# A tiled key projection ahead of the scores, its eviction ahead of the last exponentials, another projection behind the maxima's transposes, and the context loaded by pieces

## The chip, the core and the metric

The kernel runs on one core of one Trainium2 chip. The metric is the device time of one execution in microseconds (us); the time given is the median of several runs. A core has five engines that run beside each other and wait for each other by semaphores: PE (TensorE, the matmuls), DVE (VectorE), ACT (ScalarE), POOL (GpSimd) and SP (SyncE, which here only starts transfers). Each engine works through its own list of instructions in order: one that waits holds up all that are behind it on its engine.

## What is computed

One layer of a Perceiver, in fp32, on 32 batches of 64 query rows of width 256 and a context of 1601 rows of width 256, 16 heads of 16:

```
x = x + cross_attention(layernorm(x), ctx)     # softmax over 1601 keys, all 32 x 16 x 64 rows of scores
x = x + span_attention(layernorm(x))           # weights exp(-soft*(pos-mean)^2), 64 positions
x = x + ffn(layernorm(x))                      # a shared gated part and two of eight experts a token
```

The cross attention holds most of the work: keys and values are projected from the context (`ctx @ wk.T + bk`, `ctx @ wv.T`), then for each head `softmax(q @ k.T / 4) @ v`.

## The kernel before

**Stages.** A short prologue loads weights and prepares batch 0. The main loop (L767) goes over 63 *halves*: half n is batch b = n // 2 and c = n % 2, that is one set of eight heads of one batch. After it come the last half, the rest of the feed-forward's first part and the experts.

**Layout.** The context lies transposed. A batch's 1601 keys are 13 blocks of 124, loaded as four pieces (`GROUPS`: blocks 0 to 3, 4 to 6, 7 to 9, 10 to 12) of 372 KB or so each into a ring of five buffers (`ct`, L146). Scores are held with keys on the partitions, in `prob`, as four pairs of heads a half (j = 0 to 3). Their maximum over the keys is found by running maxima over the 13 blocks on DVE (`mrun`, the last one writes `mx`), four transposes on PE (`pm`, L597), a reduction on DVE (`mc`, L604), and four transposes back that spread it over the partitions (`pb`, L612), which ACT copies to `mb` (L616).

**What a half does**, in the order in which the loop's body issues it. A software pipeline runs over three halves: in iteration n the values product belongs to half n-1, the subtraction of maxima and the exponentials to half n, the scores to half n+1, and the projections of keys (K0 to K3, one for each piece) and values (V0 to V6, two blocks each) to the next batch.

1. `values(n-1, 0)`: 52 matmuls (104 records) with the first two pairs of `prob`; then `exponentials(n-1, 3)`, ACT's fourth exponential of the half before.
2. `scores(n+1, 0)`: 16 matmuls, four PSUM banks; behind them `pm` of half n; DVE adds the mask (L573) and reduces `mc`.
3. `project_keys(c, 0)`: K0, two matmuls of 496 columns on PE and an eviction on ACT (L510); then `pb` and `mb`.
4. `less_maxima(n, 0)`, POOL's first subtraction (L621, 3.75 us each); `first_maxima` (ACT, L582); steps of the other stages (`run`); `values(n-1, 1)`, which needs the third and fourth exponential; running maxima on DVE.
5. `scores(n+1, 1)`; the first exponential; K1 and two value projections; the second subtraction; steps; the second exponential.
6. The third subtraction; `scores(n+1, 2)`; K2, K3 and one or two value projections, all tiled; the fourth subtraction; the third exponential; steps.

A tiled projection (`product`, L491) cuts the weights into strips of 32 columns at the four column positions of the PE array, so that the same product is 8 matmuls instead of 2.

**What sets the order.** PE, DVE, ACT and POOL run exactly in the order in which the code issues (`manual_schedule`, L733). The steps of the layer norm, the query projection and the span attention (`query_steps` L452, `span_steps` L245, `finish_steps` L706) are generators in an `agenda`; a table (`STEPS`, L232) says after how many thirds of a half each goes on. So the extra work comes in a cycle of four halves. In every fourth half ACT has, between its third exponential (L626) and the fourth, two normalisations (`xn_q`, `xn_h`, L215) and four span exponentials (L323).

**PSUM.** `mm_bank` (L108) hands out six banks in turn (`ps_x`, L395). Whoever takes a bank writes only when the last reader of the tenant six before is done. The readers are DVE for scores and ACT for projections, `pb` and the transposes.

**SP** issues transfers in order. `load_context` (L483) asks for all four pieces of batch b+1 at the start of the half (b, 0), and for the rows `x` of a later tile behind them; the pieces wait for their buffers, and `x_kept` (L382) is issued from the steps.

Of the kernel before, what the change touches and what calls it, by code (L numbers as in the profile page):

```python
# [33 lines left out]
GROUPS = [(0, 4), (4, 3), (7, 3), (10, 3)]  # L34
# [56 lines left out]
def perceiver_kernel(ctx: ExitStack, tc: tile.TileContext, a: dict[str, bass.AP], out: bass.AP):  # L91
    nc = tc.nc
    B = a["ctxT"].shape[0]
    NT = B * S
    NTILE = NT // P
# [12 lines left out]
    def mm_bank(name: str):  # L108
        return ps_mm.tile([P, 512], F32, tag="mm", name=name)
# [16 lines left out]
    def load_x(t: int):  # L126
        xs[t] = work.tile([P, D], F32, tag="x", bufs=5, name=f"x{t}")
        nc.sync.dma_start(out=xs[t], in_=a["x"][t * P : (t + 1) * P, :])
# [14 lines left out]
    def load_piece(b: int, g: int):  # L143
        c0, n = GROUPS[g]
        k0, kn = c0 * CHUNK, min(n * CHUNK, KEYS - c0 * CHUNK)
        ct = big.tile([P, 2, 4 * CHUNK], F32, tag="ct", bufs=5, name=f"ct_{b}_{g}")  # L146
        nc.sync.dma_start(
            out=ct[:, :, :kn],
            in_=a["ctxT"][b].rearrange("(c p) k -> p c k", p=P)[:, :, k0 : k0 + kn],
        )  # L150
        cts[b].append(ct)
# [328 lines left out]

        nc.gpsimd.tensor_tensor(xs[t], xs[t], bo_row, ALU.add)

    def load_context(b: int):  # L483
        for g in range(len(GROUPS)):
            load_piece(b, g)
        if b % 2 == 0 and b // 2 + 1 < NTILE:
            t = b // 2 + 1
            load_x(t)


    def product(out, lhsT, rhs, start: bool, stop: bool, tiled: bool):  # L491
        n = lhsT.shape[-1]
        for at in range(0, n, 32) if tiled else (0,):
            end = min(at + 32, n) if tiled else n
            nc.tensor.matmul(  # L495
                out[at:end], lhsT=lhsT[:, at:end], rhs=rhs, start=start, stop=stop,
                **(dict(tile_position=(0, at)) if tiled else {}),
            )
# [15 lines left out]
    def project_values(b: int, u: int, tiled: bool = False):  # L514

        blocks = range(2 * u, min(2 * u + 2, NKC))
        ps = mm_bank(f"pv_{b}_{u}")
        for n, k in enumerate(blocks):
            g = max(g for g in range(len(GROUPS)) if GROUPS[g][0] <= k)
            k0, kn = (k - GROUPS[g][0]) * CHUNK, min(CHUNK, KEYS - k * CHUNK)  # L520
            for i in range(2):
                product(
                    ps[:kn, n * D : (n + 1) * D], cts[b][g][:, i, k0 : k0 + kn], wvT[:, i, :],
                    i == 0, i == 1, tiled,
                )
        n = len(blocks)
        nc.scalar.copy(  # L527
            vs[b % 2][:kn, 2 * u : 2 * u + n, :, :DK],
            ps[:kn, : n * D].rearrange("p (n h d) -> p n h d", n=n, d=DK),
        )  # L530

    def scores(n: int, g: int, then=None, order=None):

        b, c = halves[n]
        c0, nb = SCORED[g]


        more = [mm_bank(f"psc_{b}_{c}_{g}"), spare_pvs] if nb == 5 else None
        pss = [mm_bank(f"psc_{b}_{c}_{g}_{j}") for j in range(4)]
        for r in range(nb):  # L540
            for j in range(4):
                e, s = divmod(j, 2)[::-1]
                fifth = nb == 5 and r == 4 * s
                i = 4 if fifth else r - (nb == 5 and s == 0)
                ps, at = (more[e], s) if fifth else (pss[j], i)
                if fifth and j == 2:
                    tc.add_manual_dep(nc.tensor.nop().ins, mm.ins.name, IN_TURN, reason="banks")
                k0 = (c0 + i) * CHUNK
                product = nc.tensor.matmul(  # L549
                    ps[:CHUNK, at * P : (at + 1) * P],  # L550
                    lhsT=kTs[c][32 * j : 32 * j + 32, k0 : k0 + CHUNK],
                    rhs=qbd[b // 2][32 * j : 32 * j + 32, c, b % 2, :, :],
                    start=True, stop=True, tile_position=(32 * j, 0),
                )
                if fifth and j == 1:
                    mm = product
        held = then() if then else None
        for item in (order or ORDER[g]).split():
            if item == "t":
                if held is not None:  # L560
                    maxima_of_rows(*held)
            elif item[0] == "m":
                maximum(n, int(item[1:]))
            elif item in "AB":
                k, e = c0 + 4, "AB".index(item)
                nc.vector.tensor_tensor(  # L566
                    block_of(n, k)[:, :, e, :],
                    more[e][:CHUNK, : 2 * P].rearrange("p (r q) -> p r q", r=2),
                    madd_fifth[:CHUNK, None, :].to_broadcast([CHUNK, 2, P]), ALU.add,
                )  # L570
            else:
                j = int(item)
                nc.vector.tensor_tensor(  # L573
                    pair_of(n, j)[:, c0 : c0 + 4, :].rearrange("p k (e q) -> p k e q", e=2),
                    pss[j][:CHUNK].rearrange("p (k e q) -> p k e q", k=4, e=2),
                    madd[:CHUNK, c0 : c0 + 4, None, :].to_broadcast([CHUNK, 4, 2, S]), ALU.add,
                )
# [24 lines left out]
    def maxima_of_rows(ps, col):  # L602

        nc.vector.tensor_reduce(  # L604
            col, ps[:, : 4 * CHUNK].rearrange("p (j k) -> p j k", j=4), AX.X, ALU.max
        )
# [18 lines left out]
    def exponentials(n: int, j: int):  # L625
        nc.scalar.activation(pair_of(n, j), pair_of(n, j), AF.Exp)  # L626

    def values(n: int, r: int):

        b, c = halves[n]  # L630
        v = vs[b % 2]
        for k in range(NKC):
            kn = min(CHUNK, KEYS - k * CHUNK)
            for j in range(4):
                h = 4 * r + j
                nc.tensor.matmul(  # L636
                    pvs[32 * j : 32 * j + DK + 1, c, :, r, :],
                    lhsT=v[:kn, k, 8 * c + h, :],
                    rhs=pair_of(n, h // 2)[:kn, k, (h % 2) * S : (h % 2) * S + S],
                    start=(k == 0), stop=(k == NKC - 1), tile_position=(0, 32 * j),  # L640
                )
# [119 lines left out]
    next(queries, None)  # L761
    for u in range(7):
        project_values(0, u)
    last = len(halves) - 1

    extra = {3 * last - 3: (0,), 3 * last - 2: (1, 2, 4), 3 * last - 1: (5, 6)}
    for n, (b, c) in enumerate(halves[:-1]):  # L767
        if c == 0 and b + 1 < B:
            load_context(b + 1)
        if c and b % 2 == 0 and b // 2 + 1 < NTILE:  # L770
            agenda[3 * n].append((b // 2 + 1, query_steps(b // 2 + 1)))

        def project(f, *args):
            if b + 1 < B:
                f(b + 1, *args)

        def steps(g: int):
            run(3 * n + g)
            for u in extra.get(3 * n + g, ()):
                linear_factor(u)  # L780

        def taken_off():
            turned.extend(turned_maxima(n))
            return turned

        turned: list = []
        if n:
            values(n - 1, 0)
            exponentials(n - 1, 3)
        scores(n + 1, 0, taken_off)  # L790
        project(project_keys, c, 0)
        m = maxima_along_rows(turned[1])
        less_maxima(n, 0, m, nc.gpsimd)
        held = 3 * n in held_at
        if not held:
            first_maxima(n + 1)
        run(3 * n)
        if n:
            values(n - 1, 1)
            if c == 0:  # L800
                agenda[3 * n + 1].append((b // 2, finish_steps(b - 1, 3 * n + 1)))
        for u in extra.get(3 * n, ()):
            linear_factor(u)
        if held:
            first_maxima(n + 1)
        else:
            for k in (1, 2) if c else (1, 2, 3):
                maximum(n + 1, k)

        scores(n + 1, 1, order=LATER if held else None if c else SOONER)  # L810
        exponentials(n, 0)
        project(project_keys, c, 1)
        for u in (4, 5) if c else (0, 1):
            project(project_values, u)
        less_maxima(n, 1, m, nc.gpsimd)
        steps(1)
        exponentials(n, 1)

        less_maxima(n, 2, m, nc.gpsimd)
        scores(n + 1, 2)  # L820
        project(project_keys, c, 2, True)
        project(project_keys, c, 3, True)
        for u in (3, 6) if c else (2,):
            project(project_values, u, True)
        less_maxima(n, 3, m, nc.gpsimd)
        exponentials(n, 2)
        steps(2)
# [176 lines left out]
```

## Time and profile before

| what | value |
|---|---|
| median of three runs | 1515.38 us (1514.58 to 1522.07) |
| span of the profiled execution, first to last instruction | 1515.7 us |
| TensorE clock granted over it | 0.995 |
| four halves in the middle of the loop (840.25 to 922.53) | 82.28 us |
| scores of 16 matmuls, start to start of what follows (L549) | 1.08 us |
| K0 untiled, 496 columns (L495) | 1.67 us |
| K2 and K3 tiled, 733 columns together | 2.49 us |
| a subtraction on POOL (L621), an exponential on ACT (L626) | 3.75 us, 1.59 us |
| an eviction of keys of 496 columns (L510), a copy of `mb` (L616) | 0.66 us, 0.58 us |

A row of the timeline gives start, length, engine, line, operation, output <- inputs, partitions x elements, and how many records were merged into it; in brackets, how long the engine had been idle and what ended that. A row of the table of stretches gives a stretch's bounds, its length, the busy time and count of instructions of PE, PEld (weight loads), DVE, ACT, POOL, then the granted clock, the share of the DMA engines and GB/s. A row of the waits gives who waited for whom, the sum, how often, and the longest. "Issue" is a wait for which the profile shows no releaser. On PE a matmul's record overlaps the next one's, so that I count from start to start.

### The profile page before, as it was taken

Reading aid. Unit: us, or ns where it says so; the run is one execution under the profiler, and the core shown is the slowest. Engines: PE = TensorE matmul, PEld = TensorE weight load, DVE = VectorE, ACT = ScalarE, POOL = GpSimd, SP = SyncE. Lnnn points to the kernel's source line nnn. Section 1 sums busy time; section 2 is a strip of 40 time slices with the busy share of each in tenths; the row PEclk is TensorE's granted clock in tenths of the full one; section 3 lists DMA queues with packets and bytes.
Section 4 is the critical chain, followed back from the end, with each engine's and each line's share of the span. In section 5 each row is a group of like instructions: output and inputs, shape, how many; then the busy total and the mean of one; then the engine's idle time right before and its main releaser. Section 6 shows DMA issues by size and latency. Waiting matters only on the chain.

```text
span 1515.7 us, 62949 instructions
## 1 busy us (share of the span) xinstructions
PE 1465.0 (97%) x28600; PEld 1066.5 (70%) x28600; DVE 1225.5 (81%) x2332; ACT 946.9 (62%) x1727; POOL 1120.7 (74%) x508
## 2 busy tenths in 40 slices
PE   8999999999999999999999999999999999998899
PEld 5677767777777767777777777676777677654587
DVE  4889898998989898989989898988899898873100
ACT  3565657676767657576766677575767566766411
POOL 1777787888878887878888888878788788852710
PEclk9999999999999999999999999999999999999999
DMA  5111111111111101111111111011111111005200
GB/s 174 37 45 46 46 47 46 36 50 50 50 50 50 49 25 41 47 53 37 49 50 50 50 50 49 24 43 46 54 37 48 50 50 33 3 9 160 60 29 29
DMA packets 52076, 73.82 MB, mean 49 GB/s; under 512 B 3812, under 2 KB 51040, under 8 KB 51680
## 3 DMA queue, kind: packets, MB, share of 16 engines
q1 hardware_dynamic: 50992, 69.00, 14.9%
q8 instruction: 225, 3.69, 1.0%
q10 hardware_dynamic: 816, 0.79, 0.2%
q14 instruction: 43, 0.35, 0.1%
HBM read 65.57 MB, written 4.19 MB: 46 GB/s over the span
## 4 chain that ended last, share of the span: by engine, by line
PE 76%; DVE 17%; ACT 4%; issue 2%; POOL 0%; DMA 0%; ACTq 0%; DVEq 0%; POOLq 0%
PE pk L495 20%; PE pv L495 19%; PE psc L549 10%; PE pvs L636 10%; DVE mrun L590 8%; DVE prob L573 6%; PE py L934 4%; PE pm L597 2%; PE u L665 2%; PE ph L916 2%; PE pb L612 2%; ACT qbd L474 1%; PE psa L357 1%; PE pq L466 1%; PE po L377 1%
## 5 line engine op out<-in xcount | busy, mean ns | idle before, releaser
L621 POOL TENSOR_TENSOR prob<-prob,mb 124x1664 f32<-124x1664 f32 x252 | 939.0, 3751 | 224.2 <-ACT mb L616 218.8
L573 DVE TENSOR_TENSOR prob<-psc,madd 124x512 f32<-124x512 f32 x768 | 504.0, 680 | 76.5 <-PE psc L549 76.0
L626 ACT ACTIVATE prob<-prob 124x1664 f32<-124x1664 f32 x256 | 406.9, 1591 | 185.0 <-POOL prob L621 182.0
L590 DVE TENSOR_TENSOR mrun<-prob,mrun 124x512 f32<-124x512 f32 x704 | 486.7, 691 | 33.9 <-ACT mrun L582 20.1
L495 PE MATMUL pk<-ct,wkT_sb 128*32 128x372 f32 (+1 forms) x2512 | 387.6, 489 | 8.9 <-DMA wkT_sb<-in_wkT 5.5
L495 PE MATMUL pv<-wvT_sb,ct 128*124 128x256 f32 x3524 | 381.0, 379 | 0.9 <-DVE prob L566 0.8
L495 PEld LDWEIGHTS pv<-wvT_sb,ct 128*124 128x124 f32 x3524 | 272.8, 132 | 110.4 <-issue 17.5
L549 PE MATMUL psc<-qbd,kT 32*124 32x128 f32 x6400 | 241.8, 279 | 8.3 <-issue 6.9
L495 PEld LDWEIGHTS pk<-ct,wkT_sb 128*32 128x32 f32 (+1 forms) x2512 | 148.9, 127 | 140.1 <-issue 95.5
L549 PEld LDWEIGHTS psc<-qbd,kT 32*124 32x124 f32 x6400 | 201.9, 181 | 41.8 <-issue 20.8
L636 PE MATMUL pvs<-prob,v 124*17 124x64 f32 x13312 | 213.6, 220 | 3.0 <-issue 2.8
L527 ACT COPY v<-pv 124x512 f32<-124x512 f32 (+1 forms) x224 | 124.5, 556 | 146.5 <-PE pv L495 146.1
L636 PEld LDWEIGHTS pvs<-prob,v 124*17 124x17 f32 x13312 | 196.0, 98 | 27.9 <-issue 15.7
L510 ACT ACTIVATE kT<-pk,cols 128x372 f32<-128x372 f32 (+2 forms) x256 | 145.7, 585 | 70.0 <-PE pk L495 69.7
L323 ACT ACTIVATE sc<-sc,least 128x64 f32<-128x64 f32 x256 | 85.8, 343 | 2.6 <-DVE least L319 2.5
L936 DVE SCALAR_TENSOR_TENSOR ot<-py,prob 128x256 f32<-128x256 f32 x16 | 6.8, 424 | 75.7 <-PE py L934 66.1
L665 PE MATMUL u<-xfT,sw_sb 128*128 128x512 f32 x128 | 60.9, 624 | 3.6 <-ACT prob L692 2.7
L582 ACT COPY mrun<-prob 124x512 f32<-124x512 f32 x64 | 38.2, 596 | 37.3 <-DVE soft L306 34.3
L612 PEld LDWEIGHTS pb<-cst,mc 128*124 128x124 f32 x256 | 29.4, 135 | 36.6 <-DVE mc L604 30.0
L549 PE MATMUL pvs<-qbd,kT 32*124 32x128 f32 x256 | 54.9, 294 | 0.0
L597 PE MATMUL pm<-cst,mx 124*128 124x124 f32 x256 | 41.4, 283 | 11.4 <-DVE mx L590 10.1
L323 ACT ACTIVATION_READ_ACCUMULATOR sc<-sc,least 128x1 f32 x256 | 49.9, 195 | 0.0
(126 smaller groups left out, 1220.3 us busy)
## 6 DMA issues: line engine op xcount, KB each, us to landing
ct<-in_ctxT SPq DMA_DIRECT2D x64, 372.0 KB, 3.2
ct<-in_ctxT SPq DMA_DIRECT2D x32, 496.0 KB, 5.1
ct<-in_ctxT SPq DMA_DIRECT2D x32, 361.0 KB, 3.9
w<-in_w SPq DMA_DIRECT2D x16, 256.0 KB, 7.0
x<-in_x SPq DMA_DIRECT2D x16, 128.0 KB, 2.1
x_kept<-x SPq DMA_DIRECT2D x16, 128.0 KB, 2.0
prob<-x_kept SPq DMA_DIRECT2D x8, 256.0 KB, 6.3
out<-ot SPq DMA_DIRECT2D x16, 128.0 KB, 1.9
```

What stands on the lines that cost most here:

```text
L323: nc.scalar.activation(sc[:, h, :], sc[:, h, :], AF.Exp, bias=least[:, h : h + 1], scale=-1.0, accum_out=total[:, h : h + 1],)
L495: nc.tensor.matmul(out[at:end], lhsT=lhsT[:, at:end], rhs=rhs, start=start, stop=stop, **(dict(tile_position=(0, at)) if tiled else {}),)
L510: nc.scalar.activation(kTs[c][:, k0 : k0 + kn], ps[:, :kn], AF.Identity, bias=cols[:, B_K + c : B_K + c + 1])
L527: nc.scalar.copy(vs[b % 2][:kn, 2 * u : 2 * u + n, :, :DK], ps[:kn, : n * D].rearrange("p (n h d) -> p n h d", n=n, d=DK),)
L549: product = nc.tensor.matmul(ps[:CHUNK, at * P : (at + 1) * P], lhsT=kTs[c][32 * j : 32 * j + 32, k0 : k0 + CHUNK], rhs=qbd[b // 2][32 * j ...
L573: nc.vector.tensor_tensor(pair_of(n, j)[:, c0 : c0 + 4, :].rearrange("p k (e q) -> p k e q", e=2), pss[j][:CHUNK].rearrange("p (k e q) -> ...
L590: nc.vector.tensor_tensor(dst, block_of(n, k), run, ALU.max)
L597: nc.tensor.transpose(ps[:, j * CHUNK : (j + 1) * CHUNK], m[:CHUNK, j, :], ident[:CHUNK, :CHUNK])
L621: engine.tensor_tensor(sj, sj, m[:CHUNK, j, None, :].to_broadcast([CHUNK, NKC, P]), ALU.subtract)
L626: nc.scalar.activation(pair_of(n, j), pair_of(n, j), AF.Exp)
L636: nc.tensor.matmul(pvs[32 * j : 32 * j + DK + 1, c, :, r, :], lhsT=v[:kn, k, 8 * c + h, :], rhs=pair_of(n, h // 2)[:kn, k, (h % 2) * S : ( ...
L665: nc.tensor.matmul(ps, lhsT=w[:, c, hc * P : (hc + 1) * P], rhs=xfT[:, c, :, slot], start=(c == 0), stop=(c == 1),)
```

## The change

In each half the key projection K0 is issued ahead of the first scores, in tiled form, and its eviction ahead of the fourth exponential of the half before. In its old place, between `pm` and `pb`, stands V3 where c is 1 and K1 where c is 0, untiled. K2 moves from the third part to the second, untiled, behind V4 (c = 1) or in K1's place (c = 0). Where c is 1 the second part has K1, V4, K2 and the third K3, V5, V6; where c is 0 the second has K2, V0, V1 and the third K3, V2. The context is loaded a batch earlier: the four pieces of batch 1 ahead of the loop, then piece 0 of batch b+2 at the start of (b, 0), and pieces 1, 2 and 3 in the half (b, 1), each behind the last use of the buffer that it takes over. The load of `x` stays at the start of (b, 0), now behind one piece.

```diff
-    def load_context(b: int):
-        for g in range(len(GROUPS)):
+    def piece_ahead(b: int, g: int):
+        if b < B:
             load_piece(b, g)
-        if b % 2 == 0 and b // 2 + 1 < NTILE:
-            t = b // 2 + 1
-            load_x(t)
...
+    for g in range(len(GROUPS)):
+        load_piece(1, g)
...
     for n, (b, c) in enumerate(halves[:-1]):
-        if c == 0 and b + 1 < B:
-            load_context(b + 1)
+        if c == 0:
+            piece_ahead(b + 2, 0)
+            if b % 2 == 0 and b // 2 + 1 < NTILE:
+                load_x(b // 2 + 1)
...
         if n:
             values(n - 1, 0)
+        project(project_keys, c, 0, True)
+        if n:
             exponentials(n - 1, 3)
+        if c:
+            piece_ahead(b + 2, 1)
         scores(n + 1, 0, taken_off)
-        project(project_keys, c, 0)
+        if c:
+            project(project_values, 3)
+        else:
+            project(project_keys, c, 1)
         m = maxima_along_rows(turned[1])
...
         exponentials(n, 0)
-        project(project_keys, c, 1)
-        for u in (4, 5) if c else (0, 1):
-            project(project_values, u)
+        if c:
+            project(project_keys, c, 1)
+            piece_ahead(b + 2, 2)
+            project(project_values, 4)
+            project(project_keys, c, 2)
+            piece_ahead(b + 2, 3)
+        else:
+            project(project_keys, c, 2)
+            for u in (0, 1):
+                project(project_values, u)
...
         scores(n + 1, 2)
-        project(project_keys, c, 2, True)
         project(project_keys, c, 3, True)
-        for u in (3, 6) if c else (2,):
+        for u in (5, 6) if c else (2,):
             project(project_values, u, True)
```

## The prediction

> **What bounds the kernel now.** I read the page first, then the timelines of one cycle. The page says who is full:
>
> ```profile
> span 1515.7 us, 62949 instructions
> PE 1465.0 (97%) x28600; PEld 1066.5 (70%) x28600; DVE 1225.5 (81%) x2332; ACT 946.9 (62%) x1727; POOL 1120.7 (74%) x508
> PE 76%; DVE 17%; ACT 4%; issue 2%; POOL 0%; DMA 0%; ACTq 0%; DVEq 0%; POOLq 0%
> ```
>
> PE is full. So a change gains only what PE still waits, and loses whatever new wait it gives PE. The waits of PE, longest first, leave little to gain: 10.1 us for `mx` ahead of the transposes `pm` (L597), and 6.9 + 2.8 us for nothing that semaphores show.
>
> ```profile
> PE pm L597 <- DVE mx L590: 10.1, 16, 2.4
> PE psc L549 <- issue: 6.9, 11, 1.7
> ...
> PE pvs L636 <- issue: 2.8, 3, 1.3
> ```
>
> The loop repeats every four halves (82.28 us). I cut it where the first values matmul of a half starts, call that T0, and name the halves D (840.25, odd batch, c=1), A (861.06, even, c=0), B (879.65, even, c=1), C (900.47, odd, c=0). The busy time of the engines by half:
>
> ```profile
> 861.06:879.65 18.59, 18.59 (x423) 13.32 (x416) 15.93 (x29) 11.77 (x15) 16.18 (x6) 1.00 0.19 64
> 879.65:900.47 20.82, 20.20 (x432) 14.43 (x428) 20.16 (x36) 12.78 (x22) 17.54 (x11) 1.00 0.10 24
> 900.47:922.53 22.06, 21.91 (x464) 16.73 (x460) 19.57 (x38) 18.09 (x47) 18.76 (x9) 1.00 0.19 64
> ```
>
> (length, then PE, PEld, DVE, ACT, POOL.) Only B has a PE wait of size, 0.62 us, for `mx`; C has the fullest ACT, 18.09 of 22.06. The ACT timeline from C's T0 shows it without a gap from 900.99 to 907.9:
>
> ```profile
> 900.99 1.60 ACT L626 ACTIVATE prob<-prob 124x1664 f32<-124x1664 f32 x1
> 902.49 0.59 ACT L215 ACTIVATE xn_q<-x,neg_q,rstd_q 128x256 f32<-128x256 f32 x1
> 902.98 0.59 ACT L215 ACTIVATE xn_h<-x,neg_h,rstd_h 128x256 f32<-128x256 f32 x1
> ...
> 904.79 1.58 ACT L626 ACTIVATE prob<-prob 124x1664 f32<-124x1664 f32 x1
> 906.27 0.66 ACT L510 ACTIVATE kT<-pk,cols 128x496 f32<-128x496 f32 x1
> 906.83 0.57 ACT L616 COPY mb<-pb 124x512 f32<-124x512 f32 x1
> ```
>
> Its third exponential (900.99) starts just after POOL's third subtraction, the first of the last two in this POOL row, ends (about 900.7):
>
> ```profile
> 886.94 7.43 POOL L621 TENSOR_TENSOR prob<-prob,mb 124x1664 f32<-124x1664 f32 x2 [2.74 <-ACT mb L616]
> ...
> 896.97 7.49 POOL L621 TENSOR_TENSOR prob<-prob,mb 124x1664 f32<-124x1664 f32 x2
> ```
>
> **PE's work: no change.** The same matmuls run in another order. K0 becomes tiled and K2 untiled; where c=1, V5 becomes tiled and V3 untiled. The tiled K2 and K3 take 2.49 us for 733 columns (895.40 to 897.88), 3.40 ns a column, so a tiled K0 (496 columns) takes 1.68; untiled it takes 1.67 (903.60 to 905.27). An untiled V takes 1.73 (3.45 for two), a tiled one 1.73 (919.93 to 921.66). Sum 0; I allow 0.05 us either way in 62 halves, 3 us.
> The Trainium skill, "TensorEngine Tiling (Array Packing)", Instruction Overhead, speaks against it: each matmul has about 60 cycles of overhead, and a tiled K0 is 32 records instead of 4. Estimated from it with the 2.4 GHz of "Trainium Kernel Development and Optimization", NeuronCore Architecture, the 28 more would be 0.7 us a half, 43 us in all; the two rows above give 0.01 us a half, and I go by them.
>
> **What moves against T0.** K0 now stands ahead of the first scores: `pm` is at T0 + 1.57 + 1.68 + 1.08 = 4.33 (before 2.65). Between `pm` and `pb` stands V3 (1.71) in B and D, K1 in A and C. K1's 372 columns at 3.37 ns are 1.25. In exchange, PE's work from `pb` to the next T0 shrinks by 1.71 in B and D (one V group) and by 1.25 in A and C.
>
> *(a) The wait for `mx` in B.* DVE's work from A's `pm` to B's `mx` decides it: 863.90 to 882.94, 19.04. DVE starts from the end of the scores, so it shifts with `pm`; the copy into `mrun` comes some 0.14 earlier, since K1's eviction now ends earlier than K0's did: 18.90. PE's own way from `pm` to `pm` in A is 18.41, and (b) adds to it.
>
> *(b) A new wait for `mc` in A.* In every half without a DVE delay `pb` starts 2.15 after `pm` (scores, two additions, the reduction of 0.66). K0 filled exactly that: 0.48 + 1.67. K1 fills 0.48 + 1.25 = 1.73, so `pb` waits 0.42. Then PE's way in A is 18.83, and in B `pm` waits about 0.13 instead of 0.62 or 0.69. A and B together: 18.95 against 19.09, **-0.14 a cycle**. V3 fills 2.19, so B and D don't wait.
>
> *(c) A new wait for a PSUM bank in C.* The pool `ps_x` has six banks. K0, four scores and `pm` take six; the seventh, K1 (or V3), gets K0's bank back and must wait until ACT has evicted K0. So K0's eviction, which nobody waited for early, now has a due time: T0 + 4.8.
> In A, B and D ACT reaches it in time. In D the third exponential, `z`, `vbd` and `xn_f` end at T0 + 2.74 (842.99), in A the `o2T` copy ends near T0 + 2.0, both ahead of K0's own end at T0 + 3.25. In C it stands behind the third exponential, `xn_q`, `xn_h` and four span exponentials: 904.79 - 900.99 = 3.80 from the start of that exponential. The exponential waits for POOL, and POOL is later against C's T0 than before, as follows.
> - B's `pm` at 4.46 (with the 0.13), V3 from 4.94, `pb` 6.65. T0 of C follows after 15.33 - 1.71 = 13.62, at 20.27 from B's T0.
> - `mb` in B now stands behind V3's eviction, and this behind the fourth exponential. That one starts when POOL is done with A's fourth subtraction: T0 + 4.54 before, and later by what A's `mb` came nearer to B's T0 (12.83 to 11.71), so 5.66. Its 1.5 and the eviction's 0.5 put `mb` at 7.70.
> - From `mb` to the end of POOL's third subtraction it is 900.72 - 886.28 = 14.44, so 22.14: C's T0 + 1.87 (before 0.27).
> - The exponential starts at T0 + 1.91, K0's eviction at 5.71, its end is 6.37, K1 starts near 6.45 instead of 4.81: **+1.64 a cycle**. `mc` is long there by then, so (b) costs nothing more in C.
>
> Bounds of (c): without POOL's lateness the exponential starts at T0 + 0.52 as now; K0's eviction ends at 4.98, and `pb`'s wait for `mc` hides it, which leaves 0.42. With everything on ACT 0.5 later it is 2.1. I take 1.64, since each term is a row.
>
> *(d) The next exponentials.* The fourth has 0.7 us to spare ahead of the second values in B (885.82 to 886.53) and keeps it: both move by about as much. The second exponential ends 1.27 ahead of B's T0; that shrinks by 1.12, to about 0.15, which just holds. At the end of the loop, in the half at 1278.39, only 0.62 is to spare: some 0.5 us once.
>
> *(e) The pieces of context.* SP issues them one at a time as their buffers come free, a batch ahead; by the waits of SP they wait for PE, never PE for them, and the latest has over 15 us against landings of 3.2 to 5.1 us. `load_x` and `x_kept` stand behind fewer of them. Nothing there. What may gain is fetching code: of PE's waits called "issue", those ending at 445.72, 530.38, 946.48 and 1031.36 (4.8 us in all) end with or inside the transfer of three pieces together (441.73 to 446.97, 525.17 to 530.59, 942.42 to 947.98, 1026.25 to 1031.72), and six more (265.24, 597.43, 765.06, 807.22, 1181.73, 1265.14: 4.1 us) at the end of a piece alone. After the change all go alone, four times as many: between -8.9 and +8; I take 0. The Trainium skill, "Runtime: NRT & Kernel Launch", Instruction fetch mechanics, calls a crossing "mostly hidden"; by it these waits are none, by the rows they are up to 1.7 us each.
>
> **The sum.** C has all of that ACT work in 13 cycles (halves 10 to 58): 13 x 1.64 = 21.3. Half 2 and half 6 have less of it and pay (b), 0.42 each: 0.8. The end: 0.5. A and B: 15 x -0.14 = -2.1. Together **+20.5**: the profiled execution would go from 1515.7 to 1536.2, and the median, 0.3 below that span, to **1536**. The prologue's and the tail's order stays.
>
> **Rivals.**
> 1. *POOL isn't late, K0's eviction is in time.* It must end by T0 + 5.15, so that exponential must start by T0 + 0.68. Then C pays 0.42: 13 x 0.42 + 0.8 - 2.1 = +4, and with the code fetches between 1511 and 1527: about 1520, no change. For: ACT is 62% busy and POOL idles 218.8 us for `mb`. Against: these are averages; C's rows are gapless.
> 2. *Faster.* PE's waits are what the change removes: 9.9 of the 10.1 us for `mx`, 8.9 us of fetches, and rival 1 holds, with `mc` earlier so that (b) is small: -9.9 - 8.9 + 5 = -14, **1502**. It decides for this if `pb` starts within 1.9 of `pm` in A and C. Against: 2.15 recurs in nearly every half.
> 3. *It spreads.* The 0.15 left in (d) is gone in every A, and V3 in B waits too: 0.5 to 1 more a cycle, 1543 to 1549.
>
> **Chances.** Forecast (1528 to 1542) 0.55; rival 1 0.20; rival 2 0.12; rival 3 0.13. By the sign, with 0.5% (7.6 us) as what a measurement of this kernel tells from no change: faster 0.14, same 0.20, slower 0.66. The range runs from 1510, the low end of rival 1, to 1546, inside rival 3; the likeliest case alone is 1528 to 1542.
>
> **What would show it.** In C after the change: the eviction of K0 near T0 + 5.7 behind the four span exponentials, a PE wait of K1 for it of some 1.6 us, 13 times; `pb` waiting for `mc` in A; fewer and shorter waits of `pm`; PE's busy share down to about 96%. It is wrong if K1 follows `pm` at once in C, or if POOL's third subtraction still ends by C's T0 + 0.7.

## The result, and the profile after

The changed kernel takes 1523.24 us (1521.96 to 1526.86, 10 runs) against 1517.92 (1514.58 to 1522.07, 10 runs) of the old one: a ratio of 1.0041, interval [1.0026, 1.0056]. It is slower, as forecast, but by 5.3 us and not by 20.5, and the interval lies mostly within the 0.5% that the prediction counted as no change (to which it gave 0.20). The profiled execution went from 1515.7 to 1520.7. The page of the changed kernel, its first line, the busy times and the chain that ended last:

```profile
span 1520.7 us, 62916 instructions
PE 1465.8 (96%) x28600; PEld 1057.5 (70%) x28600; DVE 1225.4 (81%) x2332; ACT 951.7 (63%) x1727; POOL 1120.7 (74%) x508
PE 56%; DVE 21%; POOL 11%; ACT 8%; issue 3%; DMA 0%; ACTq 0%; DVEq 0%; POOLq 0%
```

PE does the same work (1465.8 against 1465.0) in a longer span, and the chain now runs through POOL and ACT as well. The waits of PE in the loop alone (234 to 1280 us; who waited for whom, the sum, how often, the longest), first of the changed kernel:

```profile
PE pk L492 <- ACT kT L507: 17.5, 13, 1.4
PE pm L594 <- DVE mx L587: 2.6, 12, 0.2
PE pb L609 <- DVE mc L601: 2.0, 11, 0.2
PE psc L546 <- issue: 0.4, 1, 0.4
```

then of the old one in the same stretch:

```profile
PE psc L549 <- issue: 5.6, 9, 1.7
PE pm L597 <- DVE mx L590: 5.6, 11, 0.6
PE pvs L636 <- issue: 2.8, 3, 1.3
PE pm L597 <- issue: 1.2, 1, 1.2
PE pk L495 <- issue: 1.2, 3, 0.6
```

The 13 waits for K0's eviction are there, as forecast. But the waits without a releaser ("issue"), 10.8 us before, are all but gone. The three halves A, B and C of one cycle (bounds, length, PE, PEld, DVE, ACT, POOL, clock, DMA):

```profile
864.64:883.45 18.81, 18.63 (x424) 13.14 (x417) 16.29 (x30) 11.53 (x15) 16.60 (x7) 1.00 0.10 30
883.45:903.85 20.40, 20.18 (x433) 14.29 (x431) 19.77 (x35) 13.08 (x23) 17.20 (x11) 1.00 0.21 58
903.85:927.51 23.66, 22.17 (x464) 16.69 (x460) 20.04 (x39) 18.38 (x47) 19.84 (x9) 1.00 0.10 30
```

C is 1.6 longer (23.66 against 22.06). PE's busy time in it grew by only 0.26 (22.17 against 21.91); the rest is one wait. POOL's row, ACT's rows and PE's row show where it comes from:

```profile
901.83 7.48 POOL L618 TENSOR_TENSOR prob<-prob,mb 124x1664 f32<-124x1664 f32 x2
```

```profile
905.64 1.59 ACT L623 ACTIVATE prob<-prob 124x1664 f32<-124x1664 f32 x1 [1.16 <-POOL prob L618]
...
909.35 0.19 ACT L323 ACTIVATION_READ_ACCUMULATOR sc<-sc,least 128x1 f32 x1
909.44 0.65 ACT L507 ACTIVATE kT<-pk,cols 128x496 f32<-128x496 f32 x1
910.00 1.58 ACT L623 ACTIVATE prob<-prob 124x1664 f32<-124x1664 f32 x1
```

```profile
908.16 0.64 PE L594 MATMUL pm<-cst,mx 124*128 124x124 f32 x4
910.15 1.52 PE L492 MATMUL pk<-ct,wkT_sb 128*128 128x372 f32 x4 [1.34 <-ACT kT L507]
```

ACT waits 1.16 us for POOL's third subtraction (the first of the two merged in POOL's row, which ends near 905.6), works without a gap through the layer norm and the span exponentials, and reaches K0's eviction at 909.44; K1 starts 0.06 after that ends. In A (T0 at 864.64) the wait for `mc` is there too:

```profile
869.44 1.42 PE L492 MATMUL pk<-ct,wkT_sb 128*128 128x372 f32 x4
871.04 0.65 PE L609 MATMUL pb<-cst,mc 128*124 128x128 f32 x4 [0.18 <-DVE mc L601]
```

The loop by the four kinds of half, halves 10 to 59, in us:

| | A (12) | B (12) | C (13) | D (13) | sum |
|---|---|---|---|---|---|
| old kernel | 229.68 | 248.95 | 286.88 | 277.57 | 1043.06 |
| changed kernel | 226.47 | 245.05 | 306.76 | 270.51 | 1048.80 |
| difference | -3.21 | -3.90 | +19.88 | -7.06 | +5.74 |
| forecast | -1.7 for A and B together | | +21.3 | 0 | +19.6 |

C pays what was forecast. A, B and D gave back 14.2 us, of which the forecast had 1.7. So the question for the experiments: what took the waits without a releaser away?

What the traces say of these waits. Packets of 16 KB arrive on the instruction queue, 173 between 234 and 1280 us, some 5.9 us apart; between two of them PE issues 243 instructions in the median, so I take them for PE's code. All 16 waits without a releaser in the old kernel end 2.2 to 2.9 us after such a packet starts: 946.48 after 944.28, 1031.36 after 1028.97, 597.43 after 594.83, 1181.73 after 1178.84. Counted from the packet's end the relation is closer still: in the 14 profiles of this document there are 69 such waits in the loop, and every one ends 1.2 to 1.6 us after the end of a packet, while a moment picked at random does so in some 7% of cases. They fall where PE issues many short matmuls: a run of 256 PE instructions takes under 2.5 us at 9.2% of its places in the old kernel, at 6.6% in the changed one. And the old kernel's transfers of three pieces together (bursts: 816 packets within about 5 us) number 25 in that stretch; the changed one has none. But only 4.8 of the 10.8 us belong to waits that end inside or with a burst. Two causes offer themselves, then: fewer bursts of transfers (theory F), or an order of PE with fewer short dense stretches.

### The profile page after: what moved, and what is told of

It reads as the page before. It is cut to its first block, busy times and chain, and to the rows that moved or that the text cites. A ratio compares the mean times of both kernels' runs of the same rounds, so it can differ in the third digit from the quotient of the medians.

```text
span 1520.7 us, 62916 instructions
## 1 busy us (share of the span) xinstructions
PE 1465.8 (96%) x28600; PEld 1057.5 (70%) x28600; DVE 1225.4 (81%) x2332; ACT 951.7 (63%) x1727; POOL 1120.7 (74%) x508
## 4 chain that ended last, share of the span: by engine, by line
PE 56%; DVE 21%; POOL 11%; ACT 8%; issue 3%; DMA 0%; ACTq 0%; DVEq 0%; POOLq 0%
PE pv L492 13%; PE pk L492 13%; POOL prob L618 9%; DVE mrun L587 8%; DVE prob L570 8%; PE psc L546 7%; PE pvs L633 7%; PE py L948 4%; PE u L662 2%; ACT sc L323 2%; PE ph L930 2%; PE pb L609 2%; ACT prob L623 2%; ACT qbd L474 1%; DVE mc L601 1%
## 5 line engine op out<-in xcount | busy, mean ns | idle before, releaser
L492 PE MATMUL pk<-ct,wkT_sb 128*32 128x496 f32 (+1 forms) x2512 | 400.7, 520 | 25.0 <-ACT kT L507 17.5
L492 PE MATMUL pv<-wvT_sb,ct 128*124 128x256 f32 x3524 | 386.1, 379 | 0.6 <-DVE prob L563 0.5
L546 PE MATMUL psc<-qbd,kT 32*124 32x128 f32 x6400 | 237.9, 279 | 1.7 <-ACT qbd L474 0.9
L507 ACT ACTIVATE kT<-pk,cols 128x372 f32<-128x372 f32 (+2 forms) x256 | 150.0, 586 | 77.1 <-PE pk L492 75.2
L937 ACT ACTIVATE hT<-ph,cols 128x256 f32<-128x256 f32 x32 | 13.4, 471 | 56.3 <-PE ph L930 56.3
```

Of the source, the lines that this page charges most:

```text
L492: nc.tensor.matmul(out[at:end], lhsT=lhsT[:, at:end], rhs=rhs, start=start, stop=stop, **(dict(tile_position=(0, at)) if tiled else {}),)
L507: nc.scalar.activation(kTs[c][:, k0 : k0 + kn], ps[:, :kn], AF.Identity, bias=cols[:, B_K + c : B_K + c + 1])
L546: product = nc.tensor.matmul(ps[:CHUNK, at * P : (at + 1) * P], lhsT=kTs[c][32 * j : 32 * j + 32, k0 : k0 + CHUNK], rhs=qbd[b // 2][32 * j ...
```

## The experiments

**1. The old kernel with V3 early.** V3 is the last reader of pieces 1 and 2; while it stands last in the half, three pieces' buffers come free together.

```diff
-        for u in (4, 5) if c else (0, 1):
+        for u in (3, 4) if c else (0, 1):
...
-        for u in (3, 6) if c else (2,):
+        for u in (5, 6) if c else (2,):
```

> The kernel before, with V3 and V5 exchanged in the halves with c = 1: V3 and V4 in the second part, V5 and V6 in the third. All else, the loading code too, is as before. Theory F (bursts): the queue of SP runs ahead of PE, and the pieces 2 and 3 of the next batch wait for the release of the buffers that V3 reads last; as V3 stood last but one, they and the next piece 0 went together at the start of each batch, and PE's fetching of its code waited behind them. With V3 early the pieces go alone, PE's waits called issue (10.8 us in the loop) go to under 3, and the time to 1506 to 1511 (before: 1517.9). Rival P (it is where the code asks for the pieces): no change, 1516 to 1520. Rival S (in the changed kernel PE's new waits let its code fetch catch up): no change here either, 1516 to 1520.

Measured: 1512.31 us, ratio 0.998 [0.9968, 0.9992]. No transfer of three pieces is left, with the old loading code. The waits of PE in the loop:

```profile
...
PE psc L549 <- issue: 1.7, 5, 0.5
PE pvs L636 <- issue: 1.7, 2, 1.0
PE pk L495 <- issue: 0.2, 1, 0.2
```

Those without a releaser fall from 10.8 to 3.6, and halves 10 to 59 take 1035.88, 7.2 less. That is F's direction, but not quite its size: it had under 3 us of such waits. The total is just above F's range too; in the profiled execution the stretch from the loop's last half to the end took 198.6 us against 194.9 in the old kernel's, with no difference in the code there, but with 25 us of it at half clock against 14. So what spread the transfers was V3's new place, not the new loading code, which the second experiment shows from the other side.

**2. The changed kernel with the old loading** (`load_context` at the start of (b, 0), no `piece_ahead`), and **3. the same with V5 behind `pm` and V3 last**, which brings the bursts back:

```diff
         if c:
-            project(project_values, 3)
+            project(project_values, 5)
...
-        for u in (5, 6) if c else (2,):
+        for u in (3, 6) if c else (2,):
```

> The changed kernel with the old loading code: all four pieces of batch b+1 and x asked for at the start of (b, 0), none ahead of the loop. The order on PE, DVE, ACT and POOL is that of the changed kernel. Theory F: the pieces still go as their buffers come free, singly, so 1521 to 1526 (changed: 1523.2), with the issue waits of PE under 3 us. Rival P: the bursts and their waits come back, 1529 to 1536. Rival S: 1521 to 1526.

> As e2_old_load, and V3 and V5 exchanged in the halves with c = 1, so that V5 stands behind the maxima's transposes and V3 tiled in the third part. Theory F: three pieces go together again, PE's issue waits come back to 6 to 11 us, time 1528 to 1535. Rival P: the same as e2_old_load, which is then slow too. Rival S: as the changed kernel, 1521 to 1526.

Measured: 1524.96, ratio 1.0054 [1.0034, 1.0074], and 1524.49, ratio 1.0053 [1.0035, 1.0072]. In the second the waits without a releaser are 0.2 us: rival P falls, the place of the loading code does nothing. In the third 24 bursts are back, and such waits are still only 1.0 us:

```profile
PE pk L495 <- issue: 0.5, 1, 0.5
PE psc L549 <- issue: 0.5, 1, 0.5
```

F, as the only cause, falls too.

| waits without a releaser, 234 to 1280 us | 24 or 25 bursts | no burst |
|---|---|---|
| old order on PE | 10.8 | 3.6 |
| new order on PE | 1.0 | 0.2 and 0.4 |

The new order takes nearly all of it away, with bursts or without. Without the bursts a third is left in the old order, so they make the waits longer or more frequent, but the waits don't need them.

**4. Is it chance?** The old kernel once more; the old kernel with 32 small matmuls (128 PE instructions) ahead of the loop, which move every later instruction to another place of its packet; and the changed kernel with the same.

```diff
     pb = mm_bank("pbv")
+    for _ in range(32):
+        nc.tensor.matmul(pb[:, :8], lhsT=..., rhs=woP[:, 0, :8], start=True, stop=True)
```

> The kernel before, unchanged, for a second profile of it. If PE's waits called issue in the loop (10.8 us in the first profile) belong to the order of its instructions and transfers, they come back within 2 us and at the same places; if they are chance, they are elsewhere and of another sum.

> The kernel before with 32 more small matmuls (eight columns, overwritten afterwards) ahead of the loop, 128 more instructions on PE; only the loop from the tenth half on is compared, not the time. Theory G (the waits come where a new page of PE's code begins inside a dense stretch of short matmuls): the pages begin elsewhere, so the issue waits stand at other places and their sum differs from 10.8 us by several us, either way. Theory F (bursts of transfers alone): same places in the half, and 8 to 12 us.

> The changed kernel with the same 128 TensorE instructions ahead of the loop as in the shifted old kernel, which puts every later instruction at another place of its code page. Theory O (the changed order has fewer short dense stretches, so that a page's boundary seldom falls where TensorE overtakes its code): TensorE's waits without a releaser inside the loop stay under 2.5 us (0.4 in the changed kernel), the loop from half 10 to half 59 stays within 1 us of 1048.8, total near 1535 with the some 12 us of the added instructions. Rival L (the changed kernel was lucky in the places of its pages): 5 to 9 us of such waits come up at new places and the loop reads 1053 to 1057.

The old kernel again took 1518.31, with 9.2 us of such waits at nearly the same places (445.2, 529.9, 596.6, 946.4, 1031.0, 1180.8). Shifted it took 1525.07 (12 us of it ahead of the loop) with 7.8 us of them at other places (440.4, 704.6, 789.5, 856.9, 941.2, 1066.8); 2.6 of the 7.8 belong to waits that end inside or with a burst:

```profile
PE psc L549 <- issue: 5.0, 8, 1.4
PE pvs L636 <- issue: 2.5, 3, 1.3
...
PE pm L597 <- issue: 0.3, 1, 0.3
```

The changed kernel shifted took 1536.02 (again 12 us ahead of the loop; halves 10 to 59 1049.84) and keeps its small sum:

```profile
PE pk L492 <- ACT kT L507: 17.3, 13, 1.4
...
PE psc L546 <- issue: 0.7, 2, 0.5
```

So the places go with the position in the code and the sum with the order: theory O holds and luck (L) falls, as far as one shift of each kernel can show.

**5. One projection between the values and the scores, in the old kernel.** If dense stretches are what matters, a projection that breaks the stretch of values and scores (68 short matmuls, 136 records) should do without the rest of the change. K2, tiled, is taken from the half before and put there; in C, ACT evicts it ahead of the layer norm.

```diff
             values(n - 1, 0)
+            if halves[n - 1][0] + 1 < B:
+                project_keys(halves[n - 1][0] + 1, halves[n - 1][1], 2, True)
+            if c == 0 and b % 2:
+                run(3 * n - 1)
             exponentials(n - 1, 3)
...
-        project(project_keys, c, 2, True)
         project(project_keys, c, 3, True)
```

> The old kernel with one thing between the first values product and the first scores: the tiled projection of the third key group, taken from the end of the half before and evicted ahead of the fourth exponential (and ahead of the layer norm's work in C). The first group stays behind the maxima's transposes, the loading and the places of the value groups are the old ones. Theory D (what lets the code fetch overtake in the old order is the dense stretch of values and scores, 136 short matmuls in 2.65 us; a projection of 1.25 us between them breaks it): TensorE's waits without a releaser in the loop fall from 9.2 to 10.8 to under 4 us although transfers of three pieces together remain, the loop from half 10 to half 59 to 1033 to 1038, total 1506 to 1513. Rival B (the bursts of three transfers decide): such waits stay at 7 to 11 us, the loop at 1041 to 1044, total 1515 to 1520. Where a wait for the eviction of that group comes up at the first key group, both are higher by it.

Measured: 1511.8 us, ratio 0.9956 [0.9939, 0.9973], halves 10 to 59 1035.48, waits without a releaser 3.2 us:

```profile
PE pk L495 <- issue: 1.4, 2, 1.3
PE psc L549 <- issue: 0.8, 1, 0.8
PE pm L597 <- issue: 0.4, 1, 0.4
PE pvs L636 <- issue: 0.3, 1, 0.3
PE pvs L549 <- issue: 0.3, 1, 0.3
```

All as theory D expects. But the transfers changed with it, since K2 reads its piece later: in 9 places three pieces still go without a pause of 0.5 us, in 8 the third comes 0.5 to 0.9 us behind two, and in 9 only two go together. So it speaks for D without excluding a share of the bursts.

**6. K0's eviction first in C.** The steps of the agenda (`xn_q`, `xn_h`, the span exponentials) go behind the eviction in C:

```diff
         project(project_keys, c, 0, True)
+        if n and c == 0 and b % 2:
+            run(3 * n - 1)
         if n:
             exponentials(n - 1, 3)
...
-        steps(2)
+        if c == 0 or b % 2:
+            steps(2)
```

> The changed kernel, but on ACT in every fourth half (C) the eviction of K0 goes ahead of xn_q, xn_h and the four span exponentials. Theory (c), the due time of K0's bank: K1 in C no longer waits (13 waits of 1.35 us now), pb starts at T0 + 6.4 instead of 7.7, the four halves take 82.4 us instead of 83.7, and the time falls by 13 x 1.28 = 16.6 to 1506 to 1508. Rival: the wait only moves, to the transposes of xn_q or to the second values product for the fourth exponential: 1517 to 1523.

Measured: 1512.48 us, ratio 0.9966 [0.9952, 0.998]. PE's waits in the loop:

```profile
PE pb L609 <- DVE mc L601: 4.6, 23, 0.5
PE pm L594 <- DVE mx L587: 2.2, 10, 0.2
PE psc L546 <- issue: 0.6, 1, 0.6
...
```

The 17.5 us for the eviction are gone, C's median half falls from 23.69 to 22.46, halves 10 to 59 from 1048.80 to 1036.96, and the waits without a releaser do not come back (0.9, and 2.0 in the last kernel of experiment 9): rival S, that the new wait only hid them, falls. The total is 5 above what was expected; 3 of that lies from the loop's last half on (198.1 us against 195.2), half of it in that half itself, where the edit moves the steps too. This is the cause of the loss, taken away alone.

**7. The order of ACT, the other way round.** The changed kernel with K0's eviction behind the fourth exponential, PE's order as changed:

```diff
-        project(project_keys, c, 0, True)
         if n:
             exponentials(n - 1, 3)
+        project(project_keys, c, 0, True)
```

> The changed kernel with the eviction of the first key group behind the fourth exponential on ScalarE, where the old kernel has it, and TensorE's order as changed. Theory R (the ring of four PSUM banks makes the eviction due before the next product): TensorE then waits in all four kinds of half for that eviction, some 1.0 us in A, 2.6 in B, 1.7 more in C and 0.1 in D, 5.4 a cycle and 13 cycles, total 1580 to 1600. Rival N (the place of the eviction costs nothing, TensorE has other work meanwhile): 1518 to 1528, no new wait named for the eviction.

Measured: 1640.87 us. The waits are those of theory R (though the ring has six banks, not four), in A 1.09, in B 2.73 and in C up to 2.64 us each; over halves 10 to 59:

```profile
PE pk L492 <- ACT kT L507: 44.0, 25, 2.6
PE pv L492 <- ACT kT L507: 32.8, 12, 2.7
```

They are 59 us more than in the changed kernel, but halves 10 to 59 grew by 100, and the total lies above R's range. Most of the rest is TensorE's clock. A wait of 2.74 us in B, and the table of the microseconds behind it:

```profile
961.84 1.63 PE L492 MATMUL pv<-wvT_sb,ct 128*124 128x256 f32 x5 [2.74 <-ACT kT L507]
```

```profile
961.00:962.00 1.00, 0.17 (x1) 0.17 (x2) 0.93 (x3) 0.78 (x2) 0.00 (x0) 1.00 0.00 0
...
963.00:964.00 1.00, 1.00 (x4) 0.81 (x3) 0.00 (x0) 0.00 (x0) 0.00 (x0) 0.50 0.00 0
...
965.00:966.00 1.00, 1.00 (x5) 0.91 (x4) 0.00 (x0) 0.68 (x2) 0.00 (x0) 0.50 0.00 0
```

The granted clock (third number from the end) falls to 0.50 within 1 us after PE has resumed and stays there for 3.4 us. In B this makes a half of 25.07 out of one of 23.39. Halves 10 to 59 have 75 us at 0.50; at 1.7 us for each 3.4 that is some 37 us, an estimate. D, which has no such wait, also grew, by 0.36 each; why, no run shows. So the eviction ahead of the exponential is not an ornament of the change: without it the new place of K0 would have cost some 117 us more.

**8. K0 untiled** (`project(project_keys, c, 0)` instead of `..., True`).

> The changed kernel with K0 untiled in its new place ahead of the scores, so that PE goes from the column strips of the values to the whole array and then to the row strips of the scores. By the rows: a change of the mode costs about 0.1 us where it can be seen (3.45 us for two V groups ahead of transposes, 3.55 ahead of scores), so one more change a half is 62 x 0.1 = 6 us, and the time is 1527 to 1532 (changed: 1523.2). If a tiled matmul has an overhead of its own, the untiled one is faster: 1510 to 1520. Rival: neither shows, 1521 to 1526.

Measured: 1528.9 us, ratio 1.0058 [1.0041, 1.0074] to the old kernel. The half A takes 19.00 instead of 18.80 and D 21.00 instead of 20.81; B and C, where PE waits for DVE or ACT, are unchanged. The tiled form is the better one by 0.2 us a half in A and D, between the tiled values and scores.

**9. More work behind `pm` in C.** First V0, on top of experiment 6, with K1 in the second part; here the second values product of those halves reads two blocks that V0 has already overwritten with the next batch's values, so that this part of the computation is changed.

```diff
+        elif b % 2:
+            project(project_values, 0)
         else:
             project(project_keys, c, 1)
```

> e4_evict_first, and in the fourth halves C also V0 behind the maxima's transposes instead of K1, which goes to the second part. V0 takes 1.73 us where K1 takes 1.35, so pb no longer waits for mc there (about 0.4 us in 13 halves in e4_evict_first). Theory (b): 1512.5 - 5 = 1506 to 1509. Rival: the wait only moves, to pm in the next half or into the second values product: 1511 to 1514.

Measured: 1505.98 us, ratio 0.9913 [0.9896, 0.993], C's median half 22.06. Then with K2 behind K1 in its place, which leaves the computation as it was:

```diff
             project(project_keys, c, 1)
+            if b % 2:
+                project(project_keys, c, 2)
...
-            project(project_keys, c, 2)
+            if b % 2 == 0:
+                project(project_keys, c, 2)
```

> The kernel with the eviction of the first key group ahead of the normalizations in the third kind of half (1512.48), and in that half the third key group's projection also behind the maxima's transposes. TensorE has 1.5 us more work between the maxima's transposes and the broadcast of them. If the broadcast's wait of 0.2 us is all that is left in that half: C from 22.46 to 22.1 or 22.3, 13 times, total 1506 to 1511. If the later broadcast (1.3 us) delays GpSimd's subtraction and with it the exponentials by as much and these are due: C unchanged or up to 23.0, total 1512 to 1520.

Measured: 1505.67 us (1502.54 to 1507.4), ratio 0.9913 [0.9896, 0.9929]: faster than both kernels. C's median half is 22.32, and PE goes from `pm` to `pb` in C without a wait:

```profile
898.16 0.64 PE L594 MATMUL pm<-cst,mx 124*128 124x124 f32 x4
898.64 2.67 PE L492 MATMUL pk<-ct,wkT_sb 128*128 128x372 f32 x8
901.15 0.60 PE L609 MATMUL pb<-cst,mc 128*124 128x128 f32 x4
```

Halves 10 to 59 take 1035.35, only 1.6 less than in experiment 6. Of the 4.9 us between the two profiled executions (1505.3 and 1510.2), 2.3 lie from the loop's last half on (195.8 against 198.1) and 1.1 ahead of the tenth half; the 6.8 between the two medians isn't located further.

## Why the prediction was right in direction and wrong in size

- **PE's work: right.** Busy time 1465.8 against 1465.0. By the prediction's estimate from the Trainium skill ("TensorEngine Tiling (Array Packing)", Instruction Overhead) the tiled form would have been dearer; experiment 8 shows it 0.2 us a half cheaper in A and D. That estimate also miscounts: a tiled K0 is 16 matmul records in the profile, not 32, so the same figures give 0.3 us a half, not 0.7. The sum didn't use it.
- **(a), the wait for `mx` in B: right.** B's steady half went from 20.82 to 20.40, with 0.2 us of wait left (forecast 0.13).
- **(b), the new wait for `mc` in A: right.** `pb` starts 1.60 behind K1 (871.04 and 869.44), and K1 alone fills 1.25 (two such products take 2.51 in experiment 9): PE loses 0.35, forecast 0.42. The list of waits shows 0.18 of it, because it counts from the end of K1's record, which on PE overlaps what follows. `pb` stood 6.40 behind T0 instead of 6.48, and A took 18.80 (forecast 18.83). A and B together went from 39.23 to 39.20, so the gain of 0.14 a cycle was nearer 0.03.
- **(c), the PSUM bank in C: right.** The third exponential started at T0 + 1.79 (forecast 1.91), K0's eviction at T0 + 5.59 (5.71), K1 at T0 + 6.30 (6.45). C's difference over 13 cycles is 19.88 (21.3). Experiment 6 takes it away and 11.8 us of the loop go with it. Rival 1 is nearest in time (about 1520) and wrong in its reason: POOL is late. That the measured time fell near it is a cancellation of (c) and (e).
- **(d), the exponentials: right.** The second exponential in A keeps 0.09 (forecast 0.15), and the one wait near the end of the loop is 0.6 us (0.5).
- **(e), the pieces and the fetch of code: this is the step that failed.** The prediction said "between -8.9 and +8; I take 0". The runs showed -10.4 in the loop's waits alone (10.8 to 0.4), 4.4 of it in D and 5.5 in A, beyond its own lower bound. It had nearly the right rows (the wait that ends at 807.22 comes 2.3 behind the last data packet, not at the end of a piece), and named transfers as the cause; it missed that the new order itself, a projection between the values and the scores, works against these waits (experiments 3 and 5).
- **The size of that step is larger than the list of waits says.** Take the length that the undisturbed halves of a kind return to: A went from 18.41 (most A halves of the old kernel are disturbed; in experiment 5, 6 of 12 stand at 18.41) to 18.80, B from 20.82 to 20.40, C from 22.06 to 23.69, and D stayed at 20.81. With these alone the 50 halves would have grown by 20.8 us, close to the 19.6 of the forecast; they grew by 5.7. The 15 us between are what the disturbed halves lie above that, nearly all in the old kernel (in its D halves 7.0 us, of which the list has 4.4; one reason is the overlap of records seen in (b)). So the sum was right for the undisturbed cycle, and its miss is term (e).
- The Trainium skill ("Runtime: NRT & Kernel Launch", Instruction fetch mechanics) calls the crossing of a code page mostly hidden. If these waits are the fetch of code, that holds for the changed order (0.4 us over some 170 packets), not for the old one (10.8 and 9.2).

What stays open: that these waits are the fetch of code is read from their distance to the packets and from the shift of their places in experiment 4; no run changed the fetch itself. How the bursts and the dense stretches divide the 10 us isn't settled, since in experiment 5 the bursts became looser too.

## What to carry to other kernels

When a product is moved, look at the seventh tenant of a ring of six banks: the eviction that nobody waited for gets a due time, and on an in-order engine it is paid by whatever stands ahead of it (here the layer norm; moving that behind the eviction turned a loss of 0.4% into a gain of 0.3%). Waits that the profile lists without a releaser are worth counting as a term with its own sum: here they recurred where the tensor engine issues many short matmuls, and an order that puts a long projection into that stretch took nearly all of them away, transfers that come one at a time two thirds. A change can hold a loss and a gain of the same size, so its halves should be priced kind by kind.

## What the runs showed of the hardware that was not expected

- In experiment 7, waits of PE of 2.0 to 2.7 us were often followed by 3.4 us at half the granted clock, which adds about 1.7 us (25.07 against 23.39 in B); but after 5 of the 12 waits of 2.73 in B nothing happened (one ends at 415.00), nor after waits of 1.34 and 1.69 in the changed and the old kernel. The length of the wait alone doesn't decide it. In all 14 profiles the granted clock changes at whole multiples of 3.41 us, counted from its first drop. Cut the profiles from 60 us on into such stretches and take those at full clock: PE idled more than 2.02 us in 59 of them, and each was followed by a drop; it idled less than 1.67 us in over 5800, and none was; between these it went either way. So a wait that falls across two stretches may cost no clock. The Trainium skill ("TensorE: Matmul & The Clock Gate", Part 1: The HAM clock gate) puts the drop after at least one idle window of some 3.4 us; here a window idle for some 2 us was enough.
- The waits without a releaser end 1.2 to 1.6 us after the end of a 16 KB packet of the instruction queue, and mostly 2.2 to 2.9 us after its start (3.2 and 3.5 in two cases, where the packet itself took 1.9 and 2.0 us instead of about 1).
- The stretch from the loop's last half to the end took 192.9 to 200.2 us in the profiles, nearly the same code in all kernels, with pieces of 3 to 10 us at a clock of 0.5; that is as much as some of the differences between the loops.
